# A two-pass graph-layer kernel: the turned activations stored in one transfer per tile, row constants loaded two pairs later, and unread products ahead of the first table product

## The chip, the core and the metric

The kernel runs on one core of a Trainium2 chip. The metric is the device time of one execution in microseconds (us). The profile is one execution taken by the hardware profiler; its times count from the start of its span.

## What is computed

The input x is 128 graphs of 64 nodes with 768 features; adj holds a 0/1 link for every pair of nodes of a graph. Two layers follow each other, each x = x + layer(relu(layernorm(x))). Cut to what matters:

```python
# layer 0
h   = relu(layernorm(x))
ctx = (adj @ (h @ Wadj.T)) / deg + (adj.T @ (h @ Wrev.T)) / rdeg + h @ Wself.T      # and biases
rel = einsum(adj, E[adj]) @ Wr.T + einsum(adj.T, E[adj.T + 40]) @ Wrr.T
x   = x + ctx + rel
# layer 1
h1  = relu(layernorm(x))
p   = einsum('bni,hio->bhno', h1, W)                  # 6 heads of 128
a   = leaky(tanh(p) . w_src + (tanh(p) . w_dst).T);  a = softmax(where(adj == 0, -999, a))
f   = elu(a @ p + b)
g   = sigmoid(h1 @ H_w.T + H_b)
out = x + g * f + (1 - g) * h1
```

## The kernel before

The 8192 rows are cut into 64 tiles of 128 rows (two graphs), and the tiles into 32 pairs. There are two passes over the pairs, one for each layer. In each pass the product of a pair with the weights is done as a 3 x 3 block product with fewer multiplications: VectorE (DVE) forms signed sums of the operand blocks (`form`) and of the weight blocks (`sum_of_weights`), TensorE (PE) multiplies them in banks `pwa` to `pwd` (pass 1, L636) or `pma` to `pmd` (pass 2, L900), and DVE adds the banks to the result (L628, L630; in pass 2 L927, L929). All matmul inputs of these products are float32.

Pass 1 is written out by hand on every engine and on the DMA queue of SyncE (SP): `merged(main(p), beside(p))` takes the products of pair p as numbered steps and puts the other work in between. Three things in it matter here.

- The end of a pair. `finish(p - 1, k)` gives three pieces for each tile of the pair before, put at steps 32, 40, 44 and 49, 55, 59: statistics, `norm_and_store`, and `turn_and_store`. The last turns h1 by 32 x 32 blocks on DVE (L680) into a tile `ht` and stores it to a scratch tensor `H1D` in DRAM (L684). `ht` shares three buffers (tag `hf`) with two other tiles, so a turn waits until the store of the last `ht` has read it.
- The row constants. `row_constants` loads the attention bias to `bb` (L273), adds one to it on DVE (L274), and loads nine small pieces of an identity to `dl` (L278). In pair 1 it stands at step 74, behind the loads for pair 3.
- The last pair. `fetch` brings the weight blocks of pass 2 (L343), makes their sums on DVE, and at step 30 loads the turned tiles of pair 0 (`load_h(0)`, L334). The loads of weight blocks b01 (step 31) and b20 (step 37) stand behind it in SP's queue; b22 and b02 (step 49) behind the store of one turned tile (step 44), b12 (step 61) behind that of the next (step 59).

At the start, PE waits for the first inputs: `prep(0)` and `degrees(0)` give the first matmul (L521, bfloat16 with the block matrix `blkb`), then `table_product` (L461) makes the relation table from the loaded `wrt` while `operands` (L589) makes the first operand blocks.

Pass 2 has its order written out for PE, DVE, ScalarE (ACT) and GpSimd (POOL) in the lists ORDER and END, but not for SP: there the scheduler places the transfers. Each pair is loaded with `load(p)`, which calls `load_h(p)`: four transfers per tile, each of 32 partitions. A turned tile lies in one of six buffers (tag `x`), so three pairs can be there at once. The other transfers of pass 2 are the links (`ai`), the halved activations (`x<-hh`, L840), a swap of graph halves between partitions (`hx`, L971), and the accumulating store of the result from POOL's queue (L1088).

In the code before, a turned tile lies in DRAM as it is read, 3072 bytes in a row for each partition of a load, and is written in pieces of 32 numbers (128 bytes):

```python
ht.rearrange("p (f b i) -> p f b i", f=NQ, b=KB)            # NQ = 4 blocks of Q = 32, KB = 6
for a in range(NQ):
    nc.sync.dma_start(H1D[p][k].rearrange("i (b a n) -> a i b n", a=NQ, n=Q)[a],
                      ht[a * Q : (a + 1) * Q].rearrange("i (b n) -> i b n", n=Q))
```

Of the kernel before, what the change touches and what calls it, by code (L numbers as in the profile page):

```python
# [8 lines left out]
F32 = mybir.dt.float32  # L9
# [6 lines left out]
P = 128  # L16
# [114 lines left out]
def kernel(  # L131
# [45 lines left out]
    nc = tc.nc  # L177
    G, N, D = x.shape
# [3 lines left out]
    KB = D // P  # L182
# [5 lines left out]
    NP = NT // 2  # L188
# [24 lines left out]
    dram = ctx.enter_context(tc.tile_pool(name="dram", bufs=1, space=bass.MemoryType.DRAM))  # L213
    HHD = [dram.tile([2 * P, D], F32, name=f"hh_{p}") for p in range(NP)]
    Q = 32
    NQ = P // Q


    H1D = [[dram.tile([Q, NQ * D], F32, name=f"h1_{p}_{k}") for k in range(2)] for p in range(NP)]

    def row(v, parts):

# [57 lines left out]
    def deviation(src, to, mv):  # L280

        st = small.tile([P, 2, 6], F32, name="st")
        for i in range(2):
            nc.vector.bn_stats(st[:, i, :], src[:, i * HALF : (i + 1) * HALF])
        nc.vector.bn_aggr(mv, st.rearrange("p a b -> p (a b)"))
        ve = small.tile([P, 1], F32, name="ve")
        nc.vector.tensor_scalar(ve, mv[:, 1:2], EPS, None, op0=OP.add)  # L287
        nc.gpsimd.tensor_tensor(to[:, 0:1], ve, mhalf, op=OP.pow)  # L288

    def scaled_mean(to, mv):  # L290

        nc.vector.scalar_tensor_tensor(to[:, 1:2], mv[:, 0:1], -1.0, to[:, 0:1],  # L292
                                       op0=OP.mult, op1=OP.mult)
# [26 lines left out]
    def sum_of_weights(places, n):  # L320
        s0, x, s1, y, at = B_SUMS[n]
        if at:
            places[n] = places[at]
        return signed(places[n], s0, places[x], s1, places[y])


    H1 = {}

    def load_h(p):
        for k in range(2):  # L330
            t = 2 * p + k
            H1[t] = keep.tile([P, D], F32, name="h1", tag="x", bufs=6)
            for f in range(NQ):
                nc.sync.dma_start(H1[t][f * Q : (f + 1) * Q], H1D[p][k][:, f * D : (f + 1) * D])  # L334

    def fetch():

# [19 lines left out]
    with ExitStack() as px:  # L357
# [3 lines left out]
        pss = px.enter_context(tc.tile_pool(name="pss0", bufs=2, space=bass.MemoryType.PSUM))  # L361
# [41 lines left out]
        blkb = wa.tile([P, P], BF16, name="blkb")  # L403
# [46 lines left out]
        def scaled_rows():  # L450
            for d in range(2):
                nc.vector.tensor_mul(es[:, d, d * NV : (d + 1) * NV],
                                     et[:, d * NB + 1 : (d + 1) * NB], ids)
# [27 lines left out]
        H0, ADF, AB, CNT, CT_T, GR, WO, SUM, HF = {}, {}, {}, {}, {}, {}, {}, {}, {}  # L481
        OPS = {}

        def relu(t, to):
            h = H0[t] = work.tile([P, D], F32, name="h0")
            nc.scalar.activation(h, X[t], AF.Relu, scale=to[:, 0:1], bias=to[:, 1:2])  # L486

        def prep(p):

            af = ADF[p] = work.tile([P, 2, 2, N], F32, name="af", bufs=1)  # L490
            nc.vector.tensor_copy(af, AI[p])
            ab = AB[p] = work.tile([P, 2, 2, N], BF16, name="ab", bufs=1)
            nc.vector.tensor_copy(ab, af)
# [22 lines left out]
        def degrees(p):  # L516


            ds = pss.tile([P, 2, 512], F32, name="pb")[:, 0, : 4 * N].rearrange(
                "p (k d n) -> p k d n", k=2, d=2)  # L520
            nc.tensor.matmul(ds, blkb, AB[p], start=True, stop=True)  # L521
            rd = work.tile([P, 2, 2, N], F32, name="rd", bufs=1)
            nc.vector.tensor_scalar(rd, ds, 1.0, None, op0=OP.max)
            return rd

        def one_over(rd):
            nc.vector.reciprocal(rd, rd)
# [72 lines left out]
        def form(p, *names):  # L600

            for n in names:
                s0, x, s1, y = A_SUMS[n]
                t = OPS[p, n] = work.tile([P, KQ, 3, P], F32, name="op", bufs=17)
                signed(t, s0, OPS[p, x], s1, OPS[p, y])
# [55 lines left out]
        def finish(p, k):  # L661

            t = 2 * p + k
            to = small.tile([P, 2], F32, name="rn")

            def norm_and_store():
                scaled_mean(to, mv)
                h = HF[t] = keep.tile([P, D], F32, name="hf", bufs=3)
                nc.scalar.activation(h, X[t], AF.Relu, scale=to[:, 0:1], bias=to[:, 1:2])  # L669
                nc.gpsimd.tensor_add(X[t], X[t], h)  # L670
                nc.sync.dma_start(of[t * P : (t + 1) * P, :], X[t])
                hh = keep.tile([P, D], F32, name="hh", tag="hf", bufs=3)
                nc.scalar.activation(hh, h, AF.Identity, scale=0.5, bias=half)
                nc.sync.dma_start(HHD[p][k * P : (k + 1) * P, :], hh)

            def turn_and_store():


                ht = keep.tile([P, D], F32, name="ht", tag="hf", bufs=3)
                nc.vector.transpose(  # L680
                    ht.rearrange("p (f b i) -> p f b i", f=NQ, b=KB),
                    HF[t].rearrange("p (b f i) -> p f b i", b=KB, f=NQ))
                for a in range(NQ):
                    nc.sync.dma_start(  # L684
                        H1D[p][k].rearrange("i (b a n) -> a i b n", a=NQ, n=Q)[a],
                        ht[a * Q : (a + 1) * Q].rearrange("i (b n) -> i b n", n=Q))

            mv = small.tile([P, 2], F32, name="mv")
            return (lambda: deviation(X[t], to, mv), norm_and_store, turn_and_store)
# [3 lines left out]
        def deviations(ts):  # L693
            to = [small.tile([P, 2], F32, name="rn") for t in ts]
            mv = [small.tile([P, 2], F32, name="mv") for t in ts]
            for i, t in enumerate(ts):
                deviation(X[t], to[i], mv[i])
            return to, mv

        def mean_and_relu(t, to, mv):  # L700
            scaled_mean(to, mv)
            relu(t, to)

        prep(0)
        scaled_rows()
        rd = degrees(0)
        to, mv = deviations((0,))
        one_over(rd)
        mean_and_relu(0, to[0], mv[0])
# [11 lines left out]
        def devs(p):  # L721
            DEV[p] = deviations((2 * p, 2 * p + 1))
# [5 lines left out]
        def degrees_and_norms(p):  # L728
            rd = degrees(p)
            relus(p)  # L730
            one_over(rd)
            over_degrees(p, rd)

        def weights_sums(*names):
            for n in names:
                sum_of_weights(bw, n)
# [42 lines left out]
        def beside(p):  # L779


            ends = [f for k in range(2) for f in finish(p - 1, k)]
            steps = [(0, lambda: form(p, "f5", "f6", "f3")), (10, lambda: form(p, "f10")),
                     (18, lambda: form(p, "f11"))]
            steps += list(zip((32, 40, 44, 49, 55, 59), ends))
            if p == 1:
                steps += [(8, lambda: weights_sums("g9")), (25, lambda: weights_sums("g1")),
                          (74, row_constants)]
            if p + 1 == NP:
                return steps + fetch()  # L790
            n = p + 1
            return steps + [
                (7, lambda: prep(n)),
                (13, lambda: devs(n)),
                (20, lambda: degrees_and_norms(n)),
                (30, lambda: prep_c(n)),
                (37, lambda: ids_worth(n, 0)),
                (43, lambda: ids_sum(n, 0)),
                (46, lambda: operands(n, 1, 2)),
                (46, lambda: operands(n, 1, 1)),  # L800
                (53, lambda: form(n, "f1")),
                (56, lambda: ids_worth(n, 1)),
                (58, lambda: operands(n, 0, 0)),
                (58, lambda: operands(n, 0, 2)),
                (61, lambda: ids_sum(n, 1)),
                (64, lambda: digits(n)),
                (66, lambda: form(n, "f7", "f4")),
                (66, lambda: load(n + 1)),
                (70, lambda: operands(n, 1, 0)),
                (70, lambda: operands(n, 0, 1)),  # L810
                (77, lambda: form(n, "f8", "f9", "f2")),
                (80, lambda: count_t(n, 0)),
                (85, lambda: count_t(n, 1))]

        for p in range(NP):
            merged(main(p), beside(p) if p else first)
# [3 lines left out]
    with ExitStack() as px:  # L820
# [3 lines left out]
        pss = px.enter_context(tc.tile_pool(name="pss1", bufs=3, space=bass.MemoryType.PSUM))  # L824
# [148 lines left out]
        def keep_awake(t, n):  # L973


            for i in range(n if t == NT - 1 else 0):
                nc.tensor.matmul(PS[t][:, : H * N], idr[:, N:], de.rearrange("p h n -> p (h n)"),
                                 start=True, stop=True)
# [278 lines left out]
```

## Time and profile before

| what | value |
|---|---|
| runs | 2461.64, 2466.97, 2467.51 us (median 2466.97) |
| profiled execution | 2461.19 us, span 2459.4 us, mean granted TensorE clock 0.997 |
| PE busy | 2425.3 us (99%), 11745 matmuls |
| DVE busy | 2046.4 us (83%) |
| ACT, POOL busy | 1025.7 us (42%), 449.7 us (18%) |
| DMA packets | 310775, of which 239306 under 512 bytes; 224.58 MB |
| SP's own queue | 300722 packets, 197.52 MB, 29.9% of the time of 16 DMA engines |
| length of a pair | about 45.7 us in pass 1, 29.2 us in pass 2 |

How to read it: a busy share of 99% on PE leaves 34 us of the span in which PE did nothing; but a matmul that runs at a lower clock counts as busy too. So beside the idle time one has to look for stretches in which the same matmul takes longer. [...]

### The profile page before, as it was taken

To read this page: it belongs to the slowest core of one execution; us is meant where nothing else is said; L and a number is where in the kernel's file an instruction comes from. 1 tells how busy PE (TensorE), PEld (TensorE's weight loads), DVE (VectorE), ACT (ScalarE), POOL (GpSimd) and SP (SyncE) were. 2 spreads that over 40 slices of the span, in tenths; PEclk is the share of its full clock that TensorE was granted. 3 is DMA by queue.
4 is the path that set the end of the run, shared out by engine and by line. 5 is a ranking of instruction groups with operands and counts; after the bars stand their busy time and mean duration, and the time that the engine had idled before them with its cause. 6 is when DMAs were issued, how large, how long until landed. Compare 5 with 4: busy or idle time off the path is not lost.

```text
span 2459.4 us, 35026 instructions
## 1 busy us (share of the span) xinstructions
PE 2425.3 (99%) x11745; PEld 1688.8 (69%) x11745; DVE 2046.4 (83%) x4169; ACT 1025.7 (42%) x3399; POOL 449.7 (18%) x799
## 2 busy tenths in 40 slices
PE   8999999999999999999999998999999999999997
PEld 6888888888888888888888884444444444444445
DVE  8878788788788788788788776788999989888999
ACT  2122222222222222223122122677677777777677
POOL 1112112112112112112112112111112111111122
PEclk9999999999999999999999999999999999999999
DMA  5222322323323223223223245445444544444445
GB/s 180 55 54 73 88 54 73 88 54 83 79 54 88 73 55 91 70 54 94 67 54 101 60 116 156 101 107 120 109 112 107 113 111 114 109 106 116 114 94 101
DMA packets 310775, 224.58 MB, mean 91 GB/s; under 512 B 239306, under 2 KB 252733, under 8 KB 310594
## 3 DMA queue, kind: packets, MB, share of 16 engines
q1 hardware_dynamic: 300722, 197.52, 29.9%
q0 software_dynamic: 9728, 24.78, 6.7%
q8 instruction: 92, 1.51, 0.3%
q14 instruction: 89, 0.73, 0.1%
q10 hardware_dynamic: 144, 0.04, 0.0%
HBM read 96.07 MB, written 100.66 MB: 80 GB/s over the span
## 4 chain that ended last, share of the span: by engine, by line
PE 91%; DVE 4%; DMA 2%; ACT 1%; SPq 1%; issue 1%; POOL 0%; DVEq 0%; POOLq 0%; ACTq 0%
PE pwa L636 19%; PE pwb L636 16%; PE pma L900 13%; PE pmb L900 11%; PE pwc L636 6%; PE pwd L636 6%; PE pb L589 5%; PE pmc L900 4%; PE pmd L900 4%; PE ps L1053 2%; PE pwd L620 1%; PE ps L1035 1%; DVE weights L309 1%; ACT pr L952 1%; PE ps L1004 1%
## 5 line engine op out<-in xcount | busy, mean ns | idle before, releaser
L636 PE MATMUL pwa<-weights,op 128*128 128x256 f32 x2304 | 550.9, 384 | 9.0 <-DVE x L630 6.1
L636 PEld LDWEIGHTS pwa<-weights,op 128*128 128x128 f32 x2304 | 423.1, 191 | 72.8 <-issue 7.6
L636 PE MATMUL pwb<-weights,op 128*128 128x256 f32 x1536 | 360.8, 381 | 0.3 <-DVE x L628 0.3
L636 PEld LDWEIGHTS pwb<-weights,op 128*128 128x128 f32 x1536 | 286.6, 190 | 44.4 <-issue 6.7
L900 PE MATMUL pma<-weights,op_f 128*128 128x512 f32 x620 | 310.3, 597 | 1.2 <-DVE weights L927 0.8
L288 POOL TENSOR_TENSOR rn<-ve,mhalf 128x1 f32<-128x1 f32 x128 | 93.5, 730 | 927.3 <-DVE ve L287 900.7
L309 DVE TENSOR_TENSOR op<-op 128x768 f32<-128x768 f32 x248 | 241.3, 993 | 1.2
L952 ACT ACTIVATE pr<-pr 128x128 f32<-128x128 f32 x768 | 225.3, 296 | 24.8 <-DVE pr L942 24.7
L486 ACT ACTIVATE h<-x,rn 128x768 f32<-128x768 f32 x64 | 62.4, 1020 | 385.1 <-DVE rn L292 366.2
L669 ACT ACTIVATE hf<-x,rn 128x768 f32<-128x768 f32 x64 | 65.7, 1027 | 356.2 <-DVE rn L292 347.9
L900 PEld LDWEIGHTS pma<-weights,op_f 128*128 128x128 f32 x620 | 112.2, 190 | 138.8 <-issue 105.6
L597 ACT COPY op<-pb 128x768 f32<-128x768 f32 x160 | 121.1, 797 | 180.5 <-PE pb L589 180.3
L900 PE MATMUL pmb<-weights,op_f 128*128 128x512 f32 x372 | 193.1, 601 | 0.4 <-DVE hz L927 0.4
L636 PE MATMUL pwc<-weights,op 128*128 128x256 f32 x780 | 187.0, 383 | 0.0
L636 PE MATMUL pwd<-weights,op 128*128 128x256 f32 x768 | 176.3, 379 | 0.0
L636 PEld LDWEIGHTS pwc<-weights,op 128*128 128x128 f32 x780 | 145.6, 190 | 25.2 <-issue 6.7
L670 POOL TENSOR_TENSOR x<-x,hf 128x768 f32<-128x768 f32 x64 | 135.9, 2124 | 133.2 <-ACT hf L669 133.2
L636 PEld LDWEIGHTS pwd<-weights,op 128*128 128x128 f32 x768 | 145.8, 190 | 20.0 <-issue 0.2
L589 PE MATMUL pb<-r,h 64*128 64x192 f32 x1536 | 152.1, 337 | 0.0
L589 PEld LDWEIGHTS pb<-r,h 64*128 64x128 f32 x1536 | 123.0, 187 | 33.5 <-issue 22.7
L952 ACT ACTIVATION_READ_ACCUMULATOR pr<-pr 128x1 f32 x768 | 144.5, 188 | 0.0
L1025 ACT ACTIVATE pb<-al,mx 128x64 f32<-128x64 f32 x384 | 128.5, 337 | 12.4 <-DVE mx L1017 11.6
(208 smaller groups left out, 4128.8 us busy)
## 6 DMA issues: line engine op xcount, KB each, us to landing
x<-in_x_dram SPq DMA_DIRECT2D x64, 384.0 KB
out_dram<-x SPq DMA_DIRECT2D x64, 384.0 KB
hh<-hh SPq DMA_DIRECT2D x64, 384.0 KB
h<-ht SPq DMA_DIRECT2D x256, 96.0 KB
h<-h SPq DMA_DIRECT2D x256, 96.0 KB
x<-hh SPq DMA_DIRECT2D x64, 384.0 KB
out_dram<-f POOLq DMA_DIRECT2D x62, 384.0 KB, 4.9
hx<-weights SPq DMA_DIRECT2D x88, 192.0 KB
```

What stands on the lines that cost most here:

```text
L288: nc.gpsimd.tensor_tensor(to[:, 0:1], ve, mhalf, op=OP.pow)
L309: return (nc.vector.tensor_add if s1 == "+" else nc.vector.tensor_sub)(to, x, y)
L486: nc.scalar.activation(h, X[t], AF.Relu, scale=to[:, 0:1], bias=to[:, 1:2])
L589: nc.tensor.matmul(ps[:, g, i * 3 * N : (i + 1) * 3 * N], H0[t][s, kb * P : (kb + 1) * P], rts[p % 2][s, k].rearrange("p s n -> p (s n)"), ...
L597: nc.scalar.copy(a.rearrange("p h s (g n) -> p g (h s) n", g=GT), ps[:, :, : 6 * N].rearrange("p g (x n) -> p g x n", n=N))
L636: nc.tensor.matmul(bank[b][:, :CQ], OPS[p, an][:, q, s, :], bw[bn][:, (s * KQ + q) * CQ : (s * KQ + q + 1) * CQ], start=(first and q == s ...
L669: nc.scalar.activation(h, X[t], AF.Relu, scale=to[:, 0:1], bias=to[:, 1:2])
L670: nc.gpsimd.tensor_add(X[t], X[t], h)
L900: nc.tensor.matmul(bank[p, b], operand(p, an)[:, q, :], bw2[bn][:, 2 * q * CQ : 2 * (q + 1) * CQ], start=(first and q == 0), stop=(q == KQ ...
L952: nc.scalar.activation(PR[t][:, j, h, :], PR[t][:, j, h, :], AF.Copy, accum_out=to)
L1025: nc.scalar.activation(PB[t][:, h, :], AL[t][:, h, :], AF.Exp, bias=MX[t][:, h : h + 1], accum_out=DN[t][:, h : h + 1])
L1053: nc.tensor.matmul(po[r][o, c, :], PT[t][s, c, o], (hs if r == g else HX[t])[s, 2 * c + r, :], start=True, stop=True)
```

## The change

There are three edits. (1) `H1D` is laid out as the turned tile is, 768 rows of 128 numbers. The turn on DVE is a plain one, and one transfer of 128 partitions stores the tile, in runs of 128 numbers (512 bytes). The four loads of pass 2 pick their 32 partitions out of it, each in runs of 32 numbers (128 bytes). (2) `row_constants` moves from pair 1 to pair 3, at the same step 74. (3) 18 products of `blkb` with itself go ahead of `prep(0)` on PE, and 14 more between the degrees and the first table product; nobody reads their result. They use the buffers of `pss`.

In the built program the order of instructions on DVE, ACT and POOL stays the same but for the moved L274. PE has the 32 products more. SP has two stores instead of eight for each pair of pass 1; in pass 2 its scheduler places the loads a little differently: the steady pattern of a pair was links, 2 loads, swap, 2 loads, hh, swap, 4 loads, hh, and becomes links, 1 load, swap, 3 loads, hh, swap, 2 loads, hh, 2 loads.

```diff
-    H1D = [[dram.tile([Q, NQ * D], F32, name=f"h1_{p}_{k}") for k in range(2)] for p in range(NP)]
+    H1D = [[dram.tile([KB * P, P], F32, name=f"h1_{p}_{k}") for k in range(2)] for p in range(NP)]
...
             for f in range(NQ):
-                nc.sync.dma_start(H1[t][f * Q : (f + 1) * Q], H1D[p][k][:, f * D : (f + 1) * D])
+                nc.sync.dma_start(
+                    H1[t][f * Q : (f + 1) * Q].rearrange("i (b n) -> i b n", n=Q),
+                    H1D[p][k].rearrange("(b i) (f n) -> f i b n", i=Q, n=Q)[f])
...
-                nc.vector.transpose(
-                    ht.rearrange("p (f b i) -> p f b i", f=NQ, b=KB),
-                    HF[t].rearrange("p (b f i) -> p f b i", b=KB, f=NQ))
-                for a in range(NQ):
-                    nc.sync.dma_start(
-                        H1D[p][k].rearrange("i (b a n) -> a i b n", a=NQ, n=Q)[a],
-                        ht[a * Q : (a + 1) * Q].rearrange("i (b n) -> i b n", n=Q))
+                nc.vector.transpose(ht, HF[t])
+                nc.sync.dma_start(H1D[p][k].rearrange("(b p) n -> p b n", p=P),
+                                  ht.rearrange("p (b n) -> p b n", b=KB))
...
+        def keep_awake(n):
+            ps = pss.tile([P, 2, 512], F32, name="pb")
+            for _ in range(n):
+                nc.tensor.matmul(ps[:, 0, :P], blkb, blkb, start=True, stop=True)
+
+        keep_awake(18)
         prep(0)
         scaled_rows()
         rd = degrees(0)
+        keep_awake(14)
...
             if p == 1:
-                steps += [(8, lambda: weights_sums("g9")), (25, lambda: weights_sums("g1")),
-                          (74, row_constants)]
+                steps += [(8, lambda: weights_sums("g9")), (25, lambda: weights_sums("g1"))]
+            if p == 3:
+                steps += [(74, row_constants)]
```

## The prediction, made before the changed kernel had run

> **What bounds the kernel now.** I read the busy shares, then stretches of each pass, then every place where PE stood idle or slow. First the page, and the busy time by stretch (us, then PE, PEld, DVE, ACT, POOL; granted clock, DMA share, GB/s):
>
> ```profile
> PE 2425.3 (99%) x11745; PEld 1688.8 (69%) x11745; DVE 2046.4 (83%) x4169; ACT 1025.7 (42%) x3399; POOL 449.7 (18%) x799
> ```
> ```profile
> 752.00:936.00 184.00, 184.00 (x987) 156.09 (x986) 149.20 (x306) 44.52 (x64) 34.73 (x32) 1.00 0.28 74
> 1900.00:2080.00 180.00, 180.00 (x725) 81.14 (x724) 162.03 (x334) 128.18 (x554) 31.84 (x99) 1.00 0.48 110
> ```
>
> In the middle of both passes PE is busy without a gap at full clock. No DVE wait or transfer there is on the path, so time can come only from the few places where PE waits. There are four: the start, pair 1, the passage between the passes (1484 to 1513), and the end. The edits touch the first three. The start and pair 1, PE's and DVE's instructions in order of time (start, us, what; in brackets the idle time before and what ended it):
>
> ```profile
> 9.61 1.65 PE L589 MATMUL pb<-r,h 64*128 64x192 f32 x8
> 11.19 1.96 PE L461 MATMUL pb<-wrt,es 128*81 128x384 f32 x4
> 14.52 0.92 PE L589 MATMUL pb<-r,h 64*128 64x192 f32 x8
> 120.23 0.70 PE L636 MATMUL pwa<-weights,op 128*128 128x256 f32 x2 [2.85 <-DVE x L630]
> 120.87 4.06 PE L636 MATMUL pwa<-weights,op 128*128 128x256 f32 x10
> ```
> ```profile
> 116.89 0.23 DVE L274 TENSOR_SCALAR bb<-bb 128x128 f32<-128x128 f32 x1 [4.17 <-DMA bb<-in_b_att_dram]
> ```
>
> The same eight matmuls take 1.65 at 9.61 and 0.92 at 14.52: PE starts slow. In pair 1, DVE stands 4.17 us for the load of `bb`; the addition of bank `pwa` (L630) is queued behind it, PE waits 2.85 us for that bank, then runs ten matmuls in 4.06 us that take 2.38 in pair 2.
>
> The passage: PE's two stops, the DVE instructions that held them up, and SP's stores:
>
> ```profile
> 1486.71 4.51 PE L636 MATMUL pwa<-weights,op 128*128 128x256 f32 x12 [2.56 <-DVE x L628]
> 1497.30 4.34 PE L636 MATMUL pwa<-weights,op 128*128 128x256 f32 x12 [3.27 <-DVE x L630]
> ```
> ```profile
> 1483.11 1.23 DVE L309 TENSOR_TENSOR weights<-weights 128x1024 f32<-128x1024 f32 x1 [4.35 <-DMA weights<-in_hw_t_dram]
> 1491.83 2.48 DVE L309 TENSOR_TENSOR weights<-weights 128x1024 f32<-128x1024 f32 x2 [3.71 <-DMA weights<-in_hw_t_dram]
> ```
> ```profile
> 1474.26 2.74 SPq L684 DMA_DIRECT2D h<-ht  x4
> 1485.25 2.64 SPq L684 DMA_DIRECT2D h<-ht  x4
> ```
>
> Both stops begin with a weight block that lands late (b02, then b12), and its loads stand in SP's queue behind four stores of a turned tile.
>
> [...] 2.56 us of idle sufficed (clock 0.50 from 1487 to 1490). [...] in one 1 us stretch of stores of 128-byte runs the engines were 0.94 busy at 143 GB/s, so 128 x 16 x 0.94 / 143 = 13.5 ns a packet, against 393 GB/s on long rows. [...] the trace's packets for 256-byte rows of the links took 19.4 ns on average. [...]
>
> **The change part by part**, against the span of 2459.4. Of the listed runs one is 2.2 us longer and two are about 8; I apply the difference to their median, 2466.97.
>
> *Unread products.* [...] `blkb` is ready at 2.31, the degrees' matmul ran at 4.33: [...] if each took 0.16 they would delay DVE's `rd` and the statistics behind it by some 0.5 us. Their buffers add no wait: PE alone writes them, and the table still waits for `rd`'s reading alone. The 14 more[...] lie between 4.7 and 6.83, when `wrt` lands. PE is then warm at 9.6. The chain from 9.61 to 14.52 (operands, table, table, bias) becomes 0.85 + 1.3 + 1.3 at warm cost (from the warm rows, 0.106 and 0.325 a matmul): 3.4 instead of 4.9, so 1.5 us. ACT's `h` (8.53 to 9.56) holds the first of them, so no more. Whether PE keeps the lead depends on DVE and the weight loads: DVE idled 3.33 us for PE at 27.31, so its chain moves along; block b00 must land by 13.9 (I estimate 13.3 from 786 KB at 250 to 320 GB/s). Bounds 0.3 worse to 1.6 better. I take -1.3.
>
> *Row constants.* From the count's matmuls at 116.99 to the next `pwb` took 8.23 us in pair 1; the same stretch of pair 2 (167.53 to 170.96) took 3.43. So -4.8 if the wait vanishes. In pair 3, DVE gets there at about 208.5. SP's queue there, before, ended its x loads at 207.5; now one store instead of four (about 0.6 instead of 2.7 to 3.3) brings `bb`'s issue to 204.7, and with the 4 us of pair 1 it lands at 208.7: 0.2 us of wait. Queued behind it are three forms and the `pwa` addition, which PE's next `pwa` product waits for. DVE has slack: that addition ends at 211.6, PE wants the bank at about 213.7. The nine `dl` loads (0.67 each, 6 us on SP) have nothing behind them until the next pair's store, 25 us later. Bounds 0 to +2.0 (a full 4.1 us wait less 2.1 slack). I take 0 there.
>
> *Store and load, pass 1.* 2 transfers instead of 8 a pair. The turn should keep its 0.98 us (same 768 numbers); no row shows the plain form, but half as much again either way lies in the 9 us a pair in which DVE idles. DVE's 27 waits for `ht` (38.5 us together) go, but PE was never idle there. 0.
>
> *Store and load, steady pass 2.* A pair's loads become 6144 packets of 128 bytes for 256 of 3 KB. Now 0.48 x 29.2 x 16 = 224 engine-us of 467 a pair. At 13.5 to 19.4 ns the new packets are 83 to 119, less about 40 for the old ones: a share of 0.57 to 0.65. Loads go into a buffer when its last reader has ended: those at 1719.6 are first read near 1756. A swap at 1708.5 is read at 1736.7. SP's issues grow from 0.42 to about 0.7 us (as the stores' 0.74), 2.3 us a pair; in all its transfers take 7.1 of 29.2 us. The result's store ends by 1706, before the loads begin. 0; no gain is possible, as PE had no gap.
>
> *Passage.* Against: `load_h(0)`, eight loads ahead of b01, takes 5.3 us (13.5 ns) to 7.4 us (19.4) of the engines instead of about 2.5, so b01 lands 0.8 to 2.8 us later; DVE's `pwa` addition behind it has 2.7 us of slack to PE. For: SP gets past each store about 2.1 us sooner, and the store is 768 packets of 512 bytes instead of 3072. For b02 I get, adding up the engines' work from 1464 on, a landing 1.3 us earlier to 1.2 later; for b12, behind the second store, 0.7 to 2.3 earlier on top. A shorter second stop also spares part of its 1.6 us at half clock. -0.7 - 1.5 - 0.4 = -2.6; bounds -6 to +2.
>
> Sum: -1.3 - 4.8 + 0 - 2.6 = -8.7. Span 2450.7; median 2458.3.
>
> **Rivals.** *Little of the passage is kept:* 128-byte reads cost about 19 ns, the passage gives 0, and the start is hidden by weight loads (-0.3): -5.1, 2462. For it: DMA shares of 0.9 to 1.0 in both places. Against: PE's order at the start shows no weight wait. *More of it is kept:* the second stop goes with its slow clock (3.3 + 1.6) and the first shrinks by 1.3: -12.3, 2454.7. *The wait only moves:* `bb` lands 4 us late in pair 3 too; PE loses 2.0 and perhaps 0.8 of clock: 2461. Against it: the shorter stores ahead of it. *Slower:* loads of 128-byte pieces saturate the DMA engines in every pair of pass 2. Free are 467 - 224 + 40 = 283 engine-us for 6144 packets: it decides from 46 ns a packet on; each ns more is 0.38 us a pair, 11.5 us over 30 pairs. At 48 ns: -8.7 + 23, 2481. For it: no row shows such reads. Against: 256-byte ones took 19.4. That nothing changes is excluded, as the built order shows each edit.
>
> **How the numbers follow.** Forecast 0.40, little kept 0.20, more kept 0.17, wait moves 0.09, slower 0.14. A measurement of this kernel can tell about 0.3% (7.4 us, so 2459.6) from no change. The forecast's own spread puts 0.33 of its 0.40 below that, 0.07 above. Faster 0.33 + 0.17 = 0.50; same 0.07 + 0.20 + 0.09 = 0.36; slower 0.14. The range takes in all but the slower case and the tails of the others: 2451 to 2468.
>
> **What would show it.** Right: eight matmuls at 9.6 in 0.9 us; no DVE wait at `bb` in pair 1 and under 0.5 us in pair 3; stretches of pass 2 with PE full and a DMA share near 0.6; a second stop under 2 us. Wrong: PE idle in the middle of pass 2 on L900 or L1053 with a DMA named; a first stop longer than 2.56 with b01 or b02 named.

## The result, and the profile after

| | before | changed |
|---|---|---|
| runs, us | 2459.08, 2461.64, 2466.97, 2467.51 | 2452.32, 2452.42, 2452.91, 2453.80 |
| median, us | 2464.3 | 2452.66 |
| profiled execution: span, us | 2459.4 | 2450.6 |
| DMA packets, MB | 310775, 224.58 | 348660, 224.54 |

The ratio is 0.9956, interval 0.9935 to 0.9976: the change makes the kernel faster, by 8.8 us between the two profiled spans. A second thing is in the first row: the four times of before lie 8 us apart, those of the changed kernel 1.5.

The traces' records of packets show what the last row counts. Both have 196608 packets of 128 bytes, 64 tiles of 3072 runs of 32 numbers: as many as the stores of before have runs, and the loads of the changed kernel. Packets of 512 bytes went from 1664 to 50816, by 64 x 768, the runs of the new stores; those of 3072 bytes from 57861 to 49669, by 64 x 128, the rows of the old loads.

The busy shares, and the same two stretches as before (us, then PE, PEld, DVE, ACT, POOL; clock, DMA share, GB/s):

```profile
PE 2424.8 (99%) x11777; PEld 1689.8 (69%) x11777; DVE 2047.8 (84%) x4169; ACT 1025.6 (42%) x3399; POOL 449.2 (18%) x799
```
```profile
752.00:936.00 184.00, 184.00 (x986) 156.12 (x985) 148.10 (x302) 44.41 (x64) 34.73 (x32) 1.00 0.22 73
1900.00:2080.00 180.00, 180.00 (x742) 81.09 (x741) 161.65 (x338) 129.15 (x566) 31.95 (x102) 1.00 0.56 110
```

PE is still without a gap in both. The DMA share fell from 0.28 to 0.22 in pass 1 and rose from 0.48 to 0.56 in pass 2; nobody pays for that, and nobody gains. The start of the changed kernel in the order of time:

```profile
2.36 2.10 PE L707 MATMUL pb<-blkb 128*128 128x128 bf16 x18 [2.36 <-DVE blkb L409]
...
4.51 1.65 PE L707 MATMUL pb<-blkb 128*128 128x128 bf16 x14
6.77 2.82 PE L463 MATMUL pb<-wrt,es 128*81 128x384 f32 x4 [0.60 <-DVE st L284]
9.96 1.54 PE L591 MATMUL pb<-r,h 64*128 64x192 f32 x8 [0.37 <-ACT h L488]
11.42 1.52 PE L463 MATMUL pb<-wrt,es 128*81 128x384 f32 x4
```

The table at 6.77 still takes 2.82, the eight products 1.54: the trace's record of the granted clock has PE at full clock from 11.25 on (before: from 12.12; the views count the time ahead of that record's first entry as full clock), and the first `pwa` product starts at 15.17 (before: 15.37). Pair 1, and `bb` in its new place in pair 3:

```profile
116.78 0.39 PE L622 MATMUL pwb<-tab,cntT 126*128 126x256 bf16 x2
...
119.76 0.39 PE L622 MATMUL pwa<-tab,cntT 126*128 126x256 bf16 x2
...
120.20 2.75 PE L638 MATMUL pwb<-weights,op 128*128 128x256 f32 x12
```
```profile
204.39 0.23 DVE L274 TENSOR_SCALAR bb<-bb 128x128 f32<-128x128 f32 x1 [0.86 <-DMA bb<-in_b_att_dram]
```

From the count to the next `pwb` it is 3.42 us instead of 8.23; in pair 3 DVE waits 0.86 and the same stretch of PE (208.26 to 211.69) stays at 3.43. The passage, PE's stops, DVE's waits and SP's stores with the first loads behind each:

```profile
1481.47 4.54 PE L638 MATMUL pwa<-weights,op 128*128 128x256 f32 x12 [2.33 <-DVE x L630]
1490.35 2.86 PE L638 MATMUL pwa<-weights,op 128*128 128x256 f32 x12 [1.52 <-DVE x L632]
1494.28 1.12 PE L908 MATMUL pmd<-weights,h 128*128 128x512 f32 x2 [0.63 <-DVE x L630]
```
```profile
1467.97 1.23 DVE L307 SCALAR_TENSOR_TENSOR weights<-weights 128x1024 f32<-128x1024 f32 x1 [4.29 <-DMA weights<-in_hw_t_dram]
1477.86 1.22 DVE L309 TENSOR_TENSOR weights<-weights 128x1024 f32<-128x1024 f32 x1 [2.92 <-DMA weights<-in_hw_t_dram]
1484.88 2.48 DVE L309 TENSOR_TENSOR weights<-weights 128x1024 f32<-128x1024 f32 x2 [2.00 <-DMA weights<-in_hw_t_dram]
```
```profile
1458.42 4.86 SPq L334 DMA_DIRECT2D h<-h  x8
1463.38 0.57 SPq L345 DMA_DIRECT2D weights<-in_w_cat_dram  x1
...
1470.44 0.37 SPq L683 DMA_DIRECT2D h<-ht  x1
1470.92 0.48 SPq L345 DMA_DIRECT2D weights<-in_w_cat_dram  x1
...
1480.00 0.37 SPq L683 DMA_DIRECT2D h<-ht  x1
1480.47 0.59 SPq L345 DMA_DIRECT2D weights<-in_w_cat_dram  x1
```

A store now holds SP for 0.37 us, not 2.7. The second stop is down from 3.27 to 1.52 and its twelve products run at full clock (2.86); the first is 2.33 for 2.56 and still costs the clock (4.54).

### The profile page after: what moved, and what is told of

Same layout as the page of the kernel before. It is cut to its first block, busy times and chain, and to the rows that moved or that the text cites. A ratio compares the mean times of both kernels' runs of the same rounds, so it can differ in the third digit from the quotient of the medians.

```text
span 2450.6 us, 34880 instructions
## 1 busy us (share of the span) xinstructions
PE 2424.8 (99%) x11777; PEld 1689.8 (69%) x11777; DVE 2047.8 (84%) x4169; ACT 1025.6 (42%) x3399; POOL 449.2 (18%) x799
## 2 busy tenths in 40 slices
DMA packets 348660, 224.54 MB, mean 92 GB/s; under 512 B 236234, under 2 KB 298813, under 8 KB 348482
## 4 chain that ended last, share of the span: by engine, by line
PE 93%; DVE 4%; ACT 1%; DMA 1%; issue 0%; SPq 0%; DVEq 0%; POOL 0%; ACTq 0%; POOLq 0%
PE pwa L638 20%; PE pwb L638 16%; PE pma L908 13%; PE pmb L908 11%; PE pwc L638 7%; PE pwd L638 7%; PE pb L591 6%; PE pmc L908 4%; PE pmd L908 4%; PE ps L1061 2%; PE pwd L622 1%; PE ps L1043 1%; DVE weights L309 1%; ACT pr L960 1%; PE ps L1012 0%
## 5 line engine op out<-in xcount | busy, mean ns | idle before, releaser
L908 PE MATMUL pma<-weights,op_f 128*128 128x512 f32 x620 | 310.3, 597 | 1.1 <-DVE weights L935 0.8
L908 PEld LDWEIGHTS pma<-weights,op_f 128*128 128x128 f32 x620 | 112.2, 190 | 138.7 <-issue 103.2
L908 PE MATMUL pmb<-weights,op_f 128*128 128x512 f32 x372 | 193.1, 601 | 0.4 <-DVE hz L935 0.4
L1033 ACT ACTIVATE pb<-al,mx 128x64 f32<-128x64 f32 x384 | 128.5, 337 | 12.4 <-DVE mx L1025 11.6
```

Of the source, the lines that this page charges most:

```text
L908: nc.tensor.matmul(bank[p, b], operand(p, an)[:, q, :], bw2[bn][:, 2 * q * CQ : 2 * (q + 1) * CQ], start=(first and q == 0), stop=(q == KQ ...
L1033: nc.scalar.activation(PB[t][:, h, :], AL[t][:, h, :], AF.Exp, bias=MX[t][:, h : h + 1], accum_out=DN[t][:, h : h + 1])
```

## The experiments

Each ratio below is to runs of the kernel before on the same chip. To set the traces beside each other I cut each span at four marks that all of them have: the first `pwa` product, pair 1's count (`pwb`, L622), the start of the last pair's f11 product (`pwd`, the one at 1468.17 in the changed kernel), and the first pass 2 product (L908). The stretch from f11 to there is called the passage. All in us, from one profiled execution each:

| kernel | to first pwa | to the count | to f11 | passage | rest | span |
|---|---|---|---|---|---|---|
| before | 15.37 | 101.62 | 1356.19 | 29.53 | 956.69 | 2459.4 |
| changed | 15.17 | 101.61 | 1351.39 | 26.11 | 956.32 | 2450.6 |
| changed, once more | 14.06 | 101.62 | 1351.39 | 28.31 | 956.42 | 2451.8 |
| rows only | 14.18 | 101.59 | 1352.35 | 31.39 | 957.39 | 2456.9 |
| layout only | 16.60 | 101.60 | 1353.24 | 29.64 | 956.82 | 2457.9 |
| products only | 14.82 | 101.66 | 1358.01 | 32.02 | 956.49 | 2463.0 |
| no products | 18.36 | 103.36 | 1351.40 | 27.22 | 956.76 | 2457.1 |
| more products | 14.32 | 101.59 | 1351.40 | 29.57 | 957.02 | 2453.9 |
| late h | 14.37 | 101.60 | 1351.40 | 26.67 | 956.86 | 2450.9 |
| 64-byte pieces | 14.29 | 101.60 | 1351.39 | 31.84 | 956.98 | 2456.1 |
| late h, b12 ahead of the store | 14.15 | 101.62 | 1351.40 | 22.27 | 956.76 | 2446.2 |

### One part at a time

**Row constants alone.**

```diff
             if p == 1:
-                steps += [(8, lambda: weights_sums("g9")), (25, lambda: weights_sums("g1")),
-                          (74, row_constants)]
+                steps += [(8, lambda: weights_sums("g9")), (25, lambda: weights_sums("g1"))]
+            if p == 3:
+                steps += [(74, row_constants)]
```

> The kernel before with one edit: row_constants at step 74 of pair 3 instead of pair 1. My theory (each part is worth what the traces of before and after show at its place): the stretch from the count's matmuls to the next pwb in pair 1 falls from 8.23 to about 3.43 us, -4.8. In pair 3 the four stores of 2.7 us still stand ahead of bb, which is issued near 202.7 instead of 200.7 and lands near 206.7; DVE gets there near 203.5 and waits about 3.2 us instead of the 0.9 of the changed kernel, of which 2.1 are slack: PE loses about 1. Sum -3.8 of the span 2459.4: 2455.6. Rival A, the move is worth the same without the new layout: DVE's wait in pair 3 is under 2.1, PE loses nothing, -4.8. Rival B, the wait only moves: PE loses 2 and the clock's part as well, -2 or less.

Measured: 2460.04 us beside 2462.66, ratio 0.9990 (0.9982 to 0.9998). DVE in pair 3, then PE there:

```profile
204.99 0.23 DVE L274 TENSOR_SCALAR bb<-bb 128x128 f32<-128x128 f32 x1 [2.47 <-DMA bb<-in_b_att_dram]
```
```profile
208.33 0.70 PE L636 MATMUL pwa<-weights,op 128*128 128x256 f32 x2 [0.69 <-DVE x L630]
```

With four stores still ahead of it, `bb` keeps DVE 2.47 us, and 0.69 of that reaches PE. The stretch to f11 is 3.84 shorter than before, 0.96 longer than in the changed kernel: my theory's "about 1", from a shorter wait than I gave (3.2) and less slack. Rival A falls. Of the 3.84 (and 1.19 at the start) the span shows 2.5, because this trace's passage is 1.86 longer than before's and its rest 0.70.

**Layout alone** (the first three hunks of the change):

> The kernel before with the new h1 layout alone (one store a tile, eight reordering loads). My theory: the passage gives about -3.3 us as in the trace of the changed kernel (first L900 product from 1502.71 to near 1499.4, less what pair 1 gives), and pair 1 gives something too, since bb is issued about 1.4 us sooner behind one store in place of four: the wait of DVE falls from 4.17 to about 2.8, PE's from 2.85 to about 1.4, and the slow clock behind it may vanish: -1.4 to -3.1. Sum -4.7 to -6.4, span 2453 to 2454.7. Rival: the parts are independent, pair 1 keeps its 8.23 us because the load's own time sets the wait, and the sum is -3.3 (2456). Rival: the 128-byte reads cost pass 2 something that the other edits cover up; then the span from the first pass 2 product to the end is over 957 us long.

Measured: 2458.7 us, ratio 0.9983 (0.9974 to 0.9991). Pair 1 did gain: DVE's wait for `bb` is 3.36 instead of 4.17, and the stretch to f11 2.95 shorter. So the parts are not independent: the shorter stores alone take 2.95 of the 4.8 us out of pair 1, and moving the row constants is then worth 1.84 (1353.24 to 1351.40, the run without products). The passage is 29.64 where I had expected some 26: no better than before's in this trace. So the span is only 1.5 shorter, not 4.7 to 6.4; the first `pwa` product also came 1.23 later than in the trace of before. The rest after it is 956.82 for before's 956.69: no cost of the 128-byte reads shows in pass 2.

**Products alone** (`keep_awake` and its two calls, nothing else):

> The kernel before with the 32 unread products alone. My theory, from the trace of the changed kernel: PE's clock comes free at about 11 instead of 12 us and the first pwa product comes 0.2 us earlier (15.17 for 15.37); nothing else moves, so -0.2 of the span, which these runs can't tell from 0. Rival (the step of the prediction): -1.3, with the eight products at 9.6 us in 0.9 us; the other edits would have had to spoil it. Rival: the products hold up the degrees and the table, +0.3.

Measured: 2463.48 us beside 2462.66, ratio 1.0001 (0.9993 to 1.0009). The first `pwa` product came 0.55 sooner, but DVE then stood 4.61 us for `bb` in pair 1 instead of 4.17: it had `bb` at 116.79 (before: 116.89), and what the start gained was waited away. More half clock followed the longer stop (the ten `pwa` products behind it took 4.58 for 4.06), and the stretch to f11 is 1.82 longer.

**The change without its products, and the changed kernel once more beside it:**

```diff
-        keep_awake(18)
         prep(0)
         scaled_rows()
         rd = degrees(0)
-        keep_awake(14)
```

> The changed kernel without its 32 unread products (new layout and moved row constants only). My theory: the products bring the first pwa product forward by 0.2 us at most when a gap of 0.6 us stands behind them, and nothing of that is to be told apart at the end: this run within 0.1% (2.5 us) of the changed kernel on the same chip, and its first pwa product at 15.2 to 15.6. Rival (the prediction's step): 1.3 us longer with the eight products at about 9.6 in 1.65 us. Rival: shorter, because the products hold up the degrees or the table.

> The changed kernel once more, on the chip and in the hour of the two that follow, to compare them with. On record it has 2452.66 beside 2464.3 of before on its first chip, a ratio of 0.9956; the run with the late h loads had the same ratio. If the ratio carries over from chip to chip: 0.9945 to 0.9965. If the passage varies with the chip (the weight block b12 has taken from 2.7 to 4.6 us to land in the traces so far), up to 0.998.

Measured, on one chip: 2453.6 us without them, ratio 0.9959 (0.9945 to 0.9972); 2454.04 with them, 0.9963 (0.9950 to 0.9975). The median doesn't feel the products, as my theory had it. The times behind the medians do: without them four executions took 2452.80 to 2453.73, the fifth, the profiled one, 2458.86; with them all five took 2452.81 to 2455.99. PE's start without, then with them:

```profile
6.46 2.82 PE L463 MATMUL pb<-wrt,es 128*81 128x384 f32 x4 [1.86 <-DVE st L284]
9.64 1.65 PE L591 MATMUL pb<-r,h 64*128 64x192 f32 x8 [0.36 <-ACT h L488]
11.22 2.85 PE L463 MATMUL pb<-wrt,es 128*81 128x384 f32 x4
...
16.78 1.65 PE L591 MATMUL pb<-r,h 64*128 64x192 f32 x8
18.36 3.75 PE L638 MATMUL pwa<-weights,op 128*128 128x256 f32 x8
22.04 0.92 PE L591 MATMUL pb<-r,h 64*128 64x192 f32 x8
```
```profile
6.30 1.49 PE L463 MATMUL pb<-wrt,es 128*81 128x384 f32 x4 [0.44 <-DVE st L284]
9.47 0.92 PE L591 MATMUL pb<-r,h 64*128 64x192 f32 x8 [1.68 <-ACT h L488]
10.32 1.52 PE L463 MATMUL pb<-wrt,es 128*81 128x384 f32 x4
```

In that execution PE worked without a gap from 9.64 to 22.04 and ran at the half-clock durations all the way; the record of the granted clock has full clock from 21.94 on, in the run beside it from 5.34. Pair 1's count came 6.04 us later than in that run (121.72 for 115.68). In the ten traces of kernels with the products full clock came by 11.25 and the first `pwa` product by 15.17; in the four without them at 9.59 to 21.94 and at 14.18 to 18.36.

The kernel before shows such a group too: of 75 executions, 19 took 2466.97 to 2470.79 and the other 56 2458.54 to 2465.05, with nothing between; of the 13 with the rows alone, three took 2464.07 to 2464.71 and the others 2460.42 at most. No kernel with both the new layout and the products has it (56 executions in nine runs, none over 3.2 us above the lowest of its run). That the upper group of before is this start is argued and not shown, since no execution of it was profiled. The size fits, and so does the mean granted clock: of the 17 for which it is on record, the 12 at 2467.24 to 2468.54 have 0.996 or 0.997, as 52 of 54 shorter ones have, so their extra time is not half clock that the record counts, and it counts none ahead of its first entry. The five from 2470.24 on have 0.995. The products alone (2460.93 to 2466.60, spread evenly) don't show the group's end as plainly.

### The start: does a gap undo the products?

```diff
-        keep_awake(14)
+        keep_awake(26)
```

> The changed kernel with 26 unread products in the second group instead of 14, so that PE has no gap before the table at 6.77 us. My theory: the clock is granted after some 4 to 5 us of work without a gap, and a gap of 0.6 us starts the count again, while one of 0.3 does not (before: gap up to 6.83, free at about 12.0; changed: gap of 0.60 up to 6.77, free at about 11.2; products alone: last gap of 0.65 up to 5.11, then one of 0.32, free at 10.1). Then the clock is free by about 8 to 9 us here, the table takes less than 2.82, the eight products at about 9.9 take 0.92 instead of 1.54 and the first pwa product comes at 13.4 to 14.2 instead of 15.17: -1 to -1.7 of the span, 2449 to 2449.6. Rival: products of this size do not count towards the clock; the table stays at 2.82 and comes up to 0.7 later: 0 to +0.7. Rival: the start gains, but a weight block that lands later takes it back: 0.

Measured: 2456.34 us, ratio 0.9970 (0.9957 to 0.9982). PE at the start:

```profile
4.51 2.42 PE L707 MATMUL pb<-blkb 128*128 128x128 bf16 x26
6.77 1.47 PE L463 MATMUL pb<-wrt,es 128*81 128x384 f32 x4
9.72 0.92 PE L591 MATMUL pb<-r,h 64*128 64x192 f32 x8 [1.48 <-ACT h L488]
```

The table at the same 6.77 now takes 1.47, and the first `pwa` product comes at 14.32. The whole is not shorter: this trace's passage is 29.57, 3.46 longer than that of the first trace of the changed kernel, and the median is 2.3 above that of the changed kernel once more (2454.04). The two ran on different chips, so whether the products or the chip lengthened the passage is open.

But that the twelve added products brought the early start is not shown. In every trace the recorded changes of the clock lie a whole number of periods of 3.413 us apart (in the changed kernel from 11.25 to 1482.40, which is 431 of them, and from there to 1485.81, one), and the place of these periods in the execution differs from trace to trace. Here full clock came at 6.24, at the end of a period that the 14 products would have filled as well but for 0.08 us (in the changed kernel they end at 6.16). In the changed kernel once more it came at 5.34, ahead of the gap of 0.44, after nothing but unread products and the degrees' matmul, all bfloat16. In the first trace the period that held the gap ended at 7.84 and was not followed by full clock; the next was, at 11.25. Whether that gap cost it the period is open: with the rows alone, a period with about as much idle (0.58 us) was followed by full clock, at 9.59.

### The passage

**h loaded late:**

```diff
-        return ([(30, lambda: load_h(0)), (67, lambda: nc.sync.dma_start(hbb, row(hb, P)))]
+        return ([(62, lambda: load_h(0)), (67, lambda: nc.sync.dma_start(hbb, row(hb, P)))]
```

> The changed kernel with the first pass 2 loads of h1 (load_h(0), eight transfers that hold SP 4.86 us) at step 62, behind b12, instead of step 30, ahead of b01. My theory: the passage is still set by when b01, b02 and b12 land. Without the eight loads ahead of it b01 is issued near 1458.6 instead of 1463.4 and lands some 4 us sooner, so DVE's wait of 4.29 us at 1467.97 is gone; b02 and b12 stand behind the tiles' stores, which follow the engines' work, so they move less (b02 about 0 to 2 us, since the engines carry 5 us less ahead of it). First stop of PE (2.33) under 1.5, second (1.52) under 1; the first L900 product 1 to 3 us earlier than 1494.28, span 2448 to 2449.5. Rival A: b02 and b12 are bound by the stores ahead of them alone and the stops stay: 0. Rival B: h then lands after 1494 and the first products of pass 2 wait for it: later by 1 to 3 us.

Measured: 2451.95 us, ratio 0.9956 (0.9944 to 0.9969), where the changed kernel has 0.9956 and 0.9963. DVE's wait for b01 is gone, and so is PE's first stop; but a single stop has taken the place of two, and the passage of 26.67 lies in the range of the changed kernel's: the 1 to 3 us that I had expected did not come. PE, DVE's waits, SP:

```profile
1487.44 5.49 PE L638 MATMUL pwa<-weights,op 128*128 128x256 f32 x12 [3.41 <-DVE x L632]
```
```profile
1474.75 1.23 DVE L309 TENSOR_TENSOR weights<-weights 128x1024 f32<-128x1024 f32 x1 [3.67 <-DMA weights<-in_hw_t_dram]
1475.89 0.97 DVE L682 STREAM_TRANSPOSE ht<-hf 128x768 f32<-128x768 f32 x1
...
1481.97 2.49 DVE L309 TENSOR_TENSOR weights<-weights 128x1024 f32<-128x1024 f32 x2 [2.20 <-DMA weights<-in_hw_t_dram]
```
```profile
1470.34 0.42 SPq L345 DMA_DIRECT2D weights<-in_hw_t_dram  x1
...
1476.89 0.37 SPq L683 DMA_DIRECT2D h<-ht  x1
1477.37 0.48 SPq L345 DMA_DIRECT2D weights<-in_w_cat_dram  x1
```

Here the loop can be read. DVE waits for b02 until 1474.75; the turn stands behind that wait, so it ends at 1476.86; the store waits for the turn (1476.89); b12's load stands behind the store (1477.37); and DVE waits for b12 at 1481.97, with the additions that PE needs behind it.

**b12 ahead of that store**, with `h` late as above. At step 50, then (second kernel) with 26 products as well, then at step 54:

```diff
-                    (49, "b22"), (49, "b02"), (61, "b12"))]
+                    (49, "b02"), (49, "b22"), (50, "b12"))]     # third kernel: (54, "b12")
```

> The run with the late h loads, and b12's two loads moved from step 61 (behind the last tile's stores) to step 50, right behind b02 and ahead of those stores. My theory: b12's place is free when the f11 product ends (1470.9), but its loads were issued at 1477.4, because they stand behind a store that waits for DVE's turn, which waits behind DVE's own wait for b02: a loop through two queues. Without it b12 lands near 1476 and DVE does not wait for it (2.20 before); the one stop that was left (3.41 and 2.7 of slow clock behind it) goes: the first L908 product at 1488.5 to 1490.5 instead of 1494.04, span 2445.5 to 2447.5. Rival A: h, loaded after b12, lands later than that and the first products of pass 2 wait for it: gain under 2. Rival B: DVE's own work (13 us of weight sums in the last 20 us of the pass) sets the stop, not b12: gain 1 or less.

> The two before together: h loads late, b12 early, and 26 unread products in the second group. If each is worth what its own theory says, the span is 1 to 1.7 us below that of the run with b12 early: 2444 to 2446.5. Rival: the start's gain is lost on the way to pair 1 (a weight block or a sum of DVE's that comes no earlier), then the span is that of b12 early within 0.5.

> The run with the late h loads, with b12's loads at step 54, behind the last reading of its place by the f11 product and still ahead of the last tile's stores (at step 50 PE had to wait 6.87 us for this load in the middle of f11). My theory: b12 is issued near 1471 instead of 1477.4 and lands near 1476, DVE's wait of 2.20 at 1481.97 goes, one stop of PE of about 1 us is left (the addition of pwa behind two weight sums) in place of 3.41 with 2.7 of slow clock behind it, and the first L908 product comes at 1488.5 to 1490.5: -3.5 to -5.5 against the changed kernel, span 2445 to 2447. Rival A: h lands too late and pass 2 waits for it: gain under 2. Rival B: the sums on DVE, not b12, set the stop: gain under 1.

In all three b12 is written over a block that the last pair has not finished reading, so that part of that pair's f11 product (step 50) or f6 product (step 54) is taken with b12's values. Measured: 2455.84 us (0.9967, 0.9955 to 0.9979), 2455.79 (0.9965, 0.9951 to 0.9979), 2454.16 (0.9961, 0.9948 to 0.9973). PE at step 50 and at step 54:

```profile
1475.13 3.78 PE L638 MATMUL pwd<-weights,op 128*128 128x256 f32 x8 [6.87 <-DMA weights<-in_w_cat_dram]
```
```profile
1475.57 5.40 PE L638 MATMUL pwa<-weights,op 128*128 128x256 f32 x12 [5.30 <-DMA weights<-in_w_cat_dram]
```

PE waits for b12's own load in the middle of the product. I had misread who reads its place last: not b10 (f11) but g5, which lies in b20's place and is read by f6. The kernel with 26 products says nothing on the start, since this wait decides both. What the three show: DVE's wait for b12 is gone when its load is ahead of the store, though PE's own stop of 5.3 to 7.2 us gave the load time as well.

**b12 behind f6, and the store behind b12**, with `h` late again:

```diff
-                    (49, "b22"), (49, "b02"), (61, "b12"))]
+                    (49, "b22"), (49, "b02"), (60, "b12"))]
...
                 nc.vector.transpose(ht, HF[t])
-                nc.sync.dma_start(H1D[p][k].rearrange("(b p) n -> p b n", p=P),
-                                  ht.rearrange("p (b n) -> p b n", b=KB))
+                HT[t] = ht
+                if t != 2 * NP - 3:
+                    store_turned(t)
...
-                return steps + fetch()
+                return steps + fetch() + [(61, lambda: store_turned(2 * NP - 3))]
```

> The run with the late h loads, with b12's loads at step 60 (right behind the f6 product, the last reader of their place: at steps 50 and 54 they came too early and PE waited for them in the middle of f11 and f6) and the turned tile's store moved behind them, to step 61; load_h(0) stays at 62. I measure the passage from the start of the f11 product (pwd) to the first pass 2 product: 29.53 us before, 26.11 and 28.31 in two traces of the changed kernel, 26.67 with the late h loads. My theory: b12 is issued near 1473.5 instead of 1477.4, because it no longer waits for the store that waits for DVE's turn that waits for b02; it lands near 1478, DVE's wait of 2.20 at 1481.97 goes, and the last stop shrinks from 3.41 to about 1 with its slow clock: a passage of 22 to 24.5 us, a span of 2446 to 2448.5. Rival A: h lands too late, and pass 2 waits for it: a passage of 25.5 or more with h named. Rival B: b12 and b02 share the DMA engines and b12 lands no sooner than before: 26 to 28.

Measured: 2448.52 us (2448.01 to 2450.76) beside 2462.65, ratio 0.9938 (0.9924 to 0.9953). PE, DVE and SP:

```profile
1485.51 2.86 PE L638 MATMUL pwa<-weights,op 128*128 128x256 f32 x12 [1.63 <-DVE x L632]
...
1489.44 1.12 PE L915 MATMUL pmd<-weights,h 128*128 128x512 f32 x2 [0.63 <-DVE x L630]
```
```profile
1480.03 2.49 DVE L309 TENSOR_TENSOR weights<-weights 128x1024 f32<-128x1024 f32 x2 [0.42 <-DMA weights<-in_hw_t_dram]
```
```profile
1475.17 0.38 SPq L345 DMA_DIRECT2D weights<-in_w_cat_dram  x1
1475.66 0.64 SPq L345 DMA_DIRECT2D weights<-in_hw_t_dram  x1
1476.74 0.37 SPq L666 DMA_DIRECT2D h<-ht  x1
1477.16 7.02 SPq L334 DMA_DIRECT2D h<-h  x8
```

b12 is issued 2.2 us sooner than with `h` late alone (I had expected some 4), DVE's wait for it is 0.42 instead of 2.20, the stop 1.63 instead of 3.41, and the record has no half clock in this passage. The passage is 22.27, 4.4 below that with `h` late alone and 3.8 to 7.4 below the five traces with the changed code there. Rivals A and B fall: `h` is there in time. Of all kernels run here this one has the lowest time, below both the kernel before and the changed one, which it did not run beside: the ratios, each to before on its own chip, are 0.9938 for 0.9956 and 0.9963.

### The slower rival: are the DMA engines near their limit in pass 2?

```diff
+                for g in range(2):
+                    s = slice(g * Q // 2, (g + 1) * Q // 2)
...
-                    H1[t][f * Q : (f + 1) * Q].rearrange("i (b n) -> i b n", n=Q),
-                    H1D[p][k].rearrange("(b i) (f n) -> f i b n", i=Q, n=Q)[f])
+                        H1[t][f * Q : (f + 1) * Q].rearrange("i (b n) -> i b n", n=Q)[:, :, s],
+                        H1D[p][k].rearrange("(b i) (f n) -> f i b n", i=Q, n=Q)[f][:, :, s])
```

> The changed kernel with each of its reordering loads split in two, so that pass 2 reads h1 in pieces of 64 bytes: 12288 packets and 16 transfers a pair instead of 6144 and 8. In the trace of the changed kernel a packet of 128 bytes takes 13.5 ns of an engine, 84 engine-us of 467 a pair. My theory: [...] 64-byte ones take about 13 as well; the DMA share of steady pass 2 rises from 0.56 to about 0.73, SP's transfers from 7 to about 12 us of 29.2, and PE stays without a gap there. At the passage load_h(0) holds SP some 4 to 5 us longer ahead of b01, and the first stop grows: 0 to +4 in all, 2450.6 to 2454.6. Rival (the slower case of the prediction, one step nearer): pieces under 128 bytes cost more than twice as much, the engines fill up and PE waits in every pair; more than 30 ns a packet would do it, and each further ns then costs 0.77 us a pair.

Measured: 2457.61 us, ratio 0.9973 (0.9962 to 0.9983). The same stretch of pass 2:

```profile
1900.00:2080.00 180.00, 180.00 (x723) 81.13 (x722) 162.05 (x334) 128.23 (x553) 32.86 (x99) 1.00 0.69 111
```

In the trace's records of packets from 1700 to 2300 us, pieces of 64 bytes took 11.1 ns on average, those of 128 bytes in the changed kernel 13.6. Twice the packets bring the share to 0.69, and PE has no gap. What this kernel loses, it loses in the passage (31.84): `load_h(0)` there holds SP 9.35 us ahead of b01 instead of 4.86. For pass 2 my theory holds (a share of 0.73 expected, some 13 ns a packet, and no gap), and the rival, which needed more than 30 ns, has no support at this size of piece. For the whole I was too low: the span of 2456.1 is 1.5 above the range I gave, which started from the trace with the shortest passage of the changed kernel.

## Why the prediction was right, and where it was not

The changed kernel is faster, and its sum of -8.7 stands beside a measured -8.8 of the span. That it meets so closely is in part luck: the second trace of the same kernel is 7.6 shorter than before's. The parts of the sum were not all what it said.

- *Row constants, -4.8 and 0.* Measured -4.8 (1356.19 to 1351.39, pair 3 included), the same in the second trace. The wait in pair 3 was 0.86, not 0.2, and hidden by the slack named. What the working did not see is that -4.8 isn't the edit's own: with the layout in place it is worth 1.8, without it 3.8. The rival of the moved wait was half right for the edit alone (PE lost 0.96 in pair 3).
- *Unread products, -1.3.* This step failed as it was put: "PE is then warm at 9.6". In the profiled execution it was not (-0.2); in the second trace it was, and brought -1.31. The chain after it was also put too short: warm, it took 3.74 (9.47 to 13.21 in that trace) for my 3.4. I treated the release of the clock as a time after work begins; that was my estimate, and no trace shows such a time. The traces have the release at anything from 5.34 to 21.94, the last after 12.3 us of gapless work at half clock, with their periods of 3.413 us in a different place each time. The products themselves took 2.10 us (18) and 1.65 (14) in the profiled execution. What the products change is not the median (2463.48 beside 2462.66 for them alone; 2453.60 without and 2454.04 with them beside the other edits) but, as far as the listed times show, the late starts.
- *Stores and loads in the steady passes, 0.* Right: to within 0.4 the rest after the passage is the same (956.69 and 956.32). The DMA share came to 0.56, just under 0.57 to 0.65, at 13.6 ns a packet for the lower end's 13.5. The upper end's 19.4, which came from packets of 256 bytes, was not reached; the 128-byte stores of before took 13.75. The slower rival needed 46.
- *Passage, -2.6.* Measured -3.4, but -1.2 in the second trace, where the second stop was 3.15 and cost the clock. Counted from f11, b01 landed 1.2 later (0.8 to 2.8 given), b02 0.2 sooner (0.7), b12 1.9 sooner (2.2). Over all traces with the same code there, four stores give 29.53, 31.39 and 32.02, one store 26.11, 27.22, 28.31, 29.57 and 29.64: means of 31.0 and 28.2, a gain of 2.8. The size was right; a single trace can't tell it to better than 2 us, since b12's load took from 2.7 to 4.65 us from the end of its issue to DVE's use.
- *From span to median.* I applied -8.7 to a median of 2466.97, because two of its three runs lay there. Those two belong to the upper group. The changed kernel has none of it, so its 2452.66 lies 5.6 below the 2458.3 forecast, while the spans differ as forecast. By the median alone the rival that keeps more of the passage (2454.7) would have looked right; its gain of 6.2 in the passage is not in the traces (3.4 and 1.2). The 8 us between the listed runs were on the table, and I did not ask what made them.

So the sum is right with two errors in it that offset each other in this execution: the start 1.1 too good, the passage 0.8 and the rest 0.4 not good enough.

## What to carry to other kernels

When a wait on a DMA sits in a queue that issues in the order written (here SP's: the store at 1476.89, b12's load behind it at 1477.37), look for the loop: engine waits for load, load stands behind a store, store waits for the engine's own work behind that wait. Breaking it, by putting the load where its place has just come free, was worth more here (4.4 us of the passage, from one trace each) than making the store cheaper (2.8, from the means). And when the listed times of a kernel lie in two groups, find out what makes the groups before setting a sum against their median.

## What the runs showed of the hardware

- In these traces the length of a stop of PE alone does not tell whether half clock followed: one of 2.33 us was followed by it, one of 2.90 was not. I cut the full-clock time of the 14 traces (three more than in the table) into periods of 3.413 us, counted from their recorded changes of the clock. All 33 periods in which PE was idle for 2.03 us or more were followed by half clock; none of the 9939 with 1.87 us or less was. The stop of 2.33 us in the changed kernel lay inside one period, and half clock followed; the one of 2.90 in its second trace was cut by the end of a period into 1.85 and 1.04, and none followed (the first two lines, then the last two; the clock is the third value from the end):

```profile
1478.98:1482.40 3.42, 1.09 (x6) 0.85 (x5) 3.42 (x5) 0.00 (x0) 0.00 (x0) 1.00 0.95 317
1482.40:1485.81 3.41, 3.41 (x9) 2.71 (x9) 1.41 (x3) 0.00 (x0) 0.00 (x0) 0.50 1.02 302
```
```profile
1476.49:1479.90 3.41, 1.55 (x9) 1.02 (x7) 2.57 (x3) 0.00 (x0) 0.69 (x1) 1.00 0.55 217
1479.90:1483.31 3.41, 2.37 (x11) 2.11 (x12) 2.45 (x4) 0.00 (x0) 0.00 (x0) 1.00 0.88 258
```

- In the passages of the eleven traces in the table, all nine stops of 3.15 us or more were followed by twelve products in 4.28 to 5.49 us instead of 2.86, none of the six of 2.09 or less was; of the seven between 2.33 and 2.90, five were and two were not (2.66, 2.90), both cut by the end of a period.
- PE stayed at half clock through 12.4 us of work without a gap, in matmuls of 64, 128 and 5 rows (9.64 to 22.04), in one of the executions. Two whole periods without a gap (11.70 to 18.53) were not followed by full clock, the third was, at 21.94. What sets the third apart is not shown.
- Between 1700 and 2300 us a packet of 64 bytes took a DMA engine 11.1 ns on average (64-byte pieces), one of 128 bytes 13.6 (changed kernel): half the bytes saved 2.5 ns.
